# Decaying attention in a fused decoder: another order of its units, of the context's keys and values, and of the loads of the experts' results

## The chip, the cores and the metric

The kernel runs on one core of one Trainium2 chip, as a single launch. The metric is the device time of the whole launch in microseconds (us), taken as a median of several runs. A profile is one further execution of the same program, recorded by the hardware profiler: it has a span (first to last recorded instruction) and a device time of its own.

A core has five engines with a queue of their own, each of which takes its instructions strictly in order: TensorE (PE: matmul; PEld is its loading of weights), VectorE (DVE), ScalarE (ACT), GpSimd (POOL) and SyncE (SP, here only for starting transfers). SBUF is the on-chip memory with 128 partitions; PSUM holds the outputs of matmuls in a few banks. A program has to wait where one engine needs what another makes, or where a buffer is still in use.

## The reference, cut to what matters

The kernel computes a decoder of four layers on x of shape 8 x 128 x 256 (8 sequences, 128 tokens, 256 features) in float32. Each layer adds an attention, a cross attention to a context of 8 x 128 x 128 and a feed-forward part, each on the layer-normed x. The change lies where layer 1's feed-forward part (experts), layer 2's attention and the preparation of layer 2's cross attention meet:

```python
x = x + _L1_ffn_ref(_layernorm(x, axis=-1), ...)      # 8 experts, 2 for each token
x = x + _L2_attn_ref(_layernorm(x, axis=-1), L2_attn_w_qkv, L2_attn_w_out, L2_attn_decay_param)
x = x + _L2_xattn_ref(_layernorm(x, axis=-1), ctx_1024, ...)
```

Layer 2's attention has no softmax. Keys and queries go through elu + 1, and the causal sums over earlier tokens decay:

```python
q = _phi(to_bhtd(q))                                  # elu(z) + 1
k = _phi(to_bhtd(k))
decay = jax.nn.sigmoid(decay_param).reshape(1, H, 1)
running_kv = _decay_scan(k * v, decay, init)          # s_t = decay * s_{t-1} + x_t
running_ksum = _decay_scan(k, decay, init)
den = jnp.clip(jnp.sum(q * running_ksum, axis=-1, keepdims=True), EPS_DEN, None)
out = q * running_kv / den                            # 16 heads of 16 features
out = out.transpose(0, 2, 1, 3).reshape(B, T, Hid) @ w_out
```

The cross attention of layer 2 needs keys (projected from the context and normalised in each head) and values (projected from the context). Neither depends on x, so both may be made at any time before that attention starts.

## The kernel before, in words

All stages run one after the other over the same x, which stays in SBUF. Where a stage has several steps for each of its units, `in_step` (L376) writes the order of work out by hand: it takes a list of (lag, function) pairs and, at step t, calls each function in the order of the list for unit t - lag. Inside it the order of the program is the order on each engine's queue. Outside it a scheduler may move instructions; `keep_in_program_order` binds one to its place.

**End of the experts (`l1_ffn`, L1200).** For each block of 128 rows TensorE makes the expert's output, VectorE scales it (`y`, L1274) and GpSimd scatters the rows to memory (`rows_out`, L1275). GpSimd also makes the row numbers for that (`to`, L1272). When all are out, `k.l2k.keys()` is called, then eight loads of 256 KB on SyncE's queue fetch each sequence's two results for every token (`y<-rows_out`), and VectorE adds both to x (`add_x`, L192). After each half of the sequences (a group g of four) the norm's statistics are taken (`norm_stats`, `ln` L155 and `ln_mv` L156) and `xn` is written (L165).

**The context's keys (`L2Keys.keys`).** GpSimd clears `va`, the store of the values, in eight memsets (L1512) and writes two columns of ones (L1514). Then for four units u (two groups x two halves of the features) TensorE projects the keys into a "mm" bank of PSUM, ScalarE adds the bias (`kc`, L1529) and squares (`sq`, L1591), TensorE sums the squares of each head, ScalarE makes the reciprocal root (Ln and Exp, L1597 and L1598), and GpSimd multiplies `kc` by it (L1536). `rest` prepares the other constants, among them `prm`, which VectorE copies from a transposed "tr" bank (L1487).

**Layer 2's attention (`l2_attn`, L1309).** It works in four units s: group g = s // 2 (512 tokens of four sequences), half o = s % 2 (128 features, eight heads) on the partitions. First come the constants: `dec`, the decay rates; `dect` (L1325), the rates spread over tokens with a zero at the start of each sequence; `heads` and `feats` (L1343), which sum over a head's features and spread back. `k.norm()` then transposes `xn` on TensorE (`ps_tr`, L183) into `xnT` (L60 on ScalarE, L62 on VectorE). For each unit:

- `project` (TensorE, matmuls in `mm`, L46): keys, values and queries into "mm" banks, of which there are four;
- `elu` (ScalarE `e` L1363 and `z` L1364, then VectorE's `k` or `q`, L1366);
- `scan` (VectorE): `kv` L1379, the scan of the keys `rks` L1380, the scan of `kv` into `rkv` L1381;
- `weigh` (VectorE): `rks` x q L1387, `rkv` x q L1388;
- `sums` (TensorE L1396): a head's sum of `rks`, the denominators, both halves of a group in one "tr" bank;
- once for a group: `inverse` (VectorE `rec` L1403 and its reciprocal L1404), `spread` (TensorE L1411), `divided` (VectorE L1416), `output` (TensorE into "o" banks, of which there are two, then `add_x`) and the statistics of the next norm.

The list that sets the order is at the end of the function. In it, `sums` of a unit comes one step late, behind the next unit's keys and values, and `k.l2k.late` turns the finished `kc` into masked keys `kb` (ScalarE, L1564) and makes the values of two sequences (TensorE, then ScalarE `va`, L1575):

```python
in_step(
    k, NC * 2,
    (0, lambda s: project(s, 1, K)), (0, keys), (0, lambda s: project(s, 2, V)),
    (1, sums), (1, last(inverse)), (0, scan),
    (0, lambda s: project(s, 0, Q)), (1, last(spread)), (0, queries), (1, last(divided)),
    (2, last(lambda g: NORM[g]())), (0, k.l2k.late), (0, weigh), (1, last(output)), (1, last(stats)),
)
```

After it the cross attention (`l2_xattn`, L1604) starts with its own norm; GpSimd adds the bias `bo` to x (L188) as soon as `xn` has been made.

Of the kernel before, what the change touches and what calls it, by code (L numbers as in the profile page):

```python
# [17 lines left out]
P = 128  # L18
B = 8
# [29 lines left out]
class Ctx:  # L49
# [71 lines left out]
    def rsqrt_begun(self, out, x):  # L121

        nc = self.nc
        t = self.sm.tile(list(x.shape), F32, name="rs_t", bufs=4)
        nc.scalar.activation(t, x, AF.Ln)
        nc.scalar.activation(out, t, AF.Exp, scale=-0.5)

        def rest():
            nc.vector.tensor_tensor(t, out, out, ALU.mult)  # L129
            nc.vector.scalar_tensor_tensor(t, t, -0.5, x, ALU.mult, ALU.mult)  # L130
            nc.vector.scalar_tensor_tensor(out, t, 1.5, out, ALU.add, ALU.mult)

        return rest
# [10 lines left out]
    def norm_stats(self, g, table=False):  # L144
# [15 lines left out]
        begun = self.rsqrt_begun(rstd, var)  # L160
# [1039 lines left out]
def l1_ffn(k):  # L1200
# [92 lines left out]
    with k.tc.tile_pool(name="l1y", bufs=1, reuse_waits="tile") as wk_:  # L1293
        Y = [wk_.tile([P, CHOICES, D], F32, name="y2", bufs=8) for _ in range(B)]
        for b in range(B):
            at = BLOCKS + CHOICES * b * S
            nc.sync.dma_start(
                Y[b], k.rows_out[at : at + CHOICES * S, :].rearrange("(p c) d -> p c d", c=CHOICES)
            )
        for g in range(2):  # L1300
# [3 lines left out]
            k.norm_stats(g)()  # L1304
# [4 lines left out]
def l2_attn(k):  # L1309
    nc, a = k.nc, k.a  # L1310
    w = k.w6
    wqkv = w[:, 0:1536].rearrange("p (c n) -> p c n", c=NC)
    wo = w[:, 1536:2048].rearrange("p (c n) -> p c n", c=NC)
    dp = w[:, 2048:2050]
    HALF = 4 * S
    with k.tc.tile_pool(name="l2a", bufs=2, reuse_waits="tile") as wk_:

        dec = k.sm.tile([P, 2], F32, name="dec")
# [3 lines left out]
        dt_ = wk_.tile([P, NC, 4, S], F32, name="dect", bufs=1)  # L1322
        nst = k.c[:, C_NST : C_NST + S].unsqueeze(1).to_broadcast([P, 4, S])
        for o in range(NC):
            nc.vector.tensor_scalar(dt_[:, o, :, :], nst, dec[:, o : o + 1], None, ALU.mult)  # L1325

        heads = wk_.tile([P, NC, 4, 32], F32, name="heads", bufs=1)
        feats = wk_.tile([P, NC, 4, P], F32, name="feats", bufs=1)
# [10 lines left out]
        own = wk_.tile([P, 4], F32, name="own4", bufs=1)  # L1339
        nc.vector.tensor_copy(own, until)  # L1340
        nc.vector.tensor_tensor(own[:, 1:4], own[:, 1:4], until[:, 0:3], ALU.subtract)
        for o in range(NC):
# [3 lines left out]
            )  # L1346
        _, xnT = k.norm()
        K, V, Q, Z, RKV, DEN, REC, PB, PY = ({} for _ in range(9))
# [10 lines left out]
        def elu(s, of, name):  # L1359

            z = of[s]
            e, z1 = tile_("e"), tile_("z1")
# [3 lines left out]
            return lambda: nc.vector.scalar_tensor_tensor(of[s], e, 1.0, z1, ALU.min, ALU.max)  # L1366

        def keys(s):
            Z[s] = elu(s, K, "k")

        def queries(s):
            Z[s] = elu(s, Q, "q")

        def scan(s):

            dd = dt_[:, s % NC].rearrange("p b s -> p (b s)")
            kv, rkv, rks = tile_("kv", 1), tile_("rkv", 4), tile_("rks")
            Z.pop(s)()
            nc.vector.tensor_tensor(kv, V.pop(s), K[s], ALU.mult)  # L1379
            nc.vector.tensor_tensor_scan(rks, dd, K.pop(s), 0.0, ALU.mult, ALU.add)  # L1380
            nc.vector.tensor_tensor_scan(rkv, dd, kv, 0.0, ALU.mult, ALU.add)  # L1381
            RKV[s] = rkv, rks

        def weigh(s):
            rkv, rks = RKV[s]
            Z.pop(s)()
            nc.vector.tensor_tensor(rks, rks, Q[s], ALU.mult)  # L1387
            nc.vector.tensor_tensor(rkv, rkv, Q.pop(s), ALU.mult)  # L1388

        def sums(s):  # L1390
            g, o = divmod(s, NC)
            rks = RKV[s][1]
            if o == 0:
                DEN[g] = k.trt((P, P))
            for j in range(4):
# [3 lines left out]
                )  # L1399

# [5 lines left out]
        def spread(g):  # L1406
            r = REC.pop(g)
            for o in range(NC):
                PB[g, o] = k.mmt()
# [3 lines left out]
        def divided(g):  # L1413
            for o in range(NC):
                rkv = RKV[2 * g + o][0]
                nc.vector.tensor_tensor(rkv, rkv, PB.pop((g, o)), ALU.mult)  # L1416

        def output(g):
            for j in range(4):
                b = 4 * g + j  # L1420
                PY[b] = k.ot()
                mm(nc, PY[b], [(RKV[2 * g + o][0][:, tok(j)], wo[:, o, :]) for o in range(NC)])
# [5 lines left out]
        def last(f):  # L1428
            return lambda s: f(s // NC) if s % NC else None

        NORM = {}
        in_step(
            k, NC * 2,
            (0, lambda s: project(s, 1, K)), (0, keys), (0, lambda s: project(s, 2, V)),
            (1, sums), (1, last(inverse)), (0, scan),
            (0, lambda s: project(s, 0, Q)), (1, last(spread)), (0, queries), (1, last(divided)),
            (2, last(lambda g: NORM[g]())), (0, k.l2k.late), (0, weigh), (1, last(output)), (1, last(stats)),
# [3 lines left out]
class L2Keys:  # L1441
# [58 lines left out]
    def keys(self):  # L1500
# [5 lines left out]
        self.pool = pool = self.inner.enter_context(k.tc.tile_pool(name="l2kt", bufs=1, reuse_waits="tile"))  # L1506

# [3 lines left out]
        for b in range(B):  # L1511
            nc.gpsimd.memset(self.va[:, b], 0.0)  # L1512
# [8 lines left out]
        RS = {}  # L1521

        def project(u):
            g, o = divmod(u, NC)
            pk = k.mmt((P, 4, S))
# [6 lines left out]
            RS[u] = l2_rstd(k, pool, self.kc[:, u].rearrange("p b s -> p (b s)"))  # L1532

        def scaled(u):
            rs = RS.pop(u)()
            nc.gpsimd.tensor_tensor(self.kc[:, u], self.kc[:, u], rs.rearrange("p (b s) -> p b s", s=S), ALU.mult)  # L1536

        in_step(k, 4, (0, project), (1, scaled))
# [30 lines left out]
    def values(self, b):  # L1569
        k = self.k  # L1570
        pv = k.ot((P, 2, D))
        for t, wv in enumerate((self.wvm, self.wvd)):
            mm(k.nc, pv[:, t, :], [(k.ctxT[:, b, :], wv)])
        for t in range(2):
            k.nc.scalar.activation(  # L1575
                self.va[:, b, :, t, 0:16], pv[:, t, :].rearrange("p (h d) -> p h d", d=16), AF.Copy, scale=self.ends[t]
            )

    def late(self, u):
        self.masked(u)  # L1580
        for b in (2 * u, 2 * u + 1):
            self.values(b)


def l2_rstd(k, pool, t, bias=None):
# [8 lines left out]
    rs = pool.tile([P, n], F32, name="rs", bufs=2)  # L1594
# [1012 lines left out]
```

## Time and profile before

| what | value |
|---|---|
| median of three runs | 1988.71 us (1983.61, 1988.71, 1989.26) |
| the profiled execution | 1987.05 us |
| its span | 1985.0 us |
| mean granted clock of TensorE | 0.928 of full speed |
| stretch that the change touches | about 880 to 963 us of the span |

The profile's page gives the busy time of each engine over the span, then the chain of work that ended last. The trace can be asked for the same in any stretch: windows (busy time of each engine, with the TensorE clock that was granted there), the chain (start in us from the span's start, length in us, engine, tile, line), and waits (which engine's instruction waited for which, in us in total, how often, longest). "issue" is time in which an engine waited for nothing that the profile shows. A busy TensorE need not be one at full clock: in this stretch the granted clock is 0.5 from 897.99 to 911.65 and from 949.19 to 959.43 us, and 1.0 in the rest of 880 to 963. One matmul of float32 with 512 columns shows as two records; a projection is four.

Mean times of single instructions there, from the groups by line:

| instruction | engine | mean |
|---|---|---|
| `e` 128x512, `z` 128x512 | ACT | 0.60, 0.69 us |
| `va` 128x256 | ACT | 0.47 us |
| `k` and other products 128x512 | DVE | 0.67 to 0.69 us alone |
| scan 128x512 | DVE | 1.20 to 1.22 us |
| reciprocal 128x128 | DVE | 0.95 us |
| add to x 128x256 | DVE | 0.42 us |
| `kc` x root 128x512 | POOL | 1.26 to 1.44 us |
| clear of `va` 128x1024 | POOL | 0.97 us |

Instructions that follow each other on VectorE overlap a little: the next one starts 0.08 to 0.1 us before the end shown.

### The profile page before, as it was taken

What the parts mean: (1) busy time and instruction counts of PE and PEld (TensorE: products, weight loads), DVE (VectorE), ACT (ScalarE), POOL (GpSimd) and SP (SyncE); (2) the same over time, 40 slices, a digit from 0 to 9 for tenths busy, and PEclk for the clock granted to TensorE, in tenths of its full rate; (3) what the DMA queues carried; (4) which work ended last, traced back from release to release, by engine and by line L of the source; (5) the groups of instructions that cost most, each with busy time, mean ns of one, the idle gap of its engine ahead of it and who ended that gap; (6) DMA issues with size and microseconds to landing.
All of it is one profiled execution on the core that took longest, in us unless ns stands there. A gap on an engine that the chain in (4) does not pass through costs nothing.

```text
span 1985.0 us, 25197 instructions
## 1 busy us (share of the span) xinstructions
PE 1724.8 (87%) x9473; PEld 1146.6 (58%) x9479; DVE 1198.6 (60%) x2376; ACT 1035.2 (52%) x1687; POOL 419.6 (21%) x415
## 2 busy tenths in 40 slices
PE   6776977758999959998678889999999996999999
PEld 3454655535666635654356645555555556888666
DVE  5766777766677742327455576776776775445433
ACT  2446844425767731234353277787777762444422
POOL 3544623110212132340143100000000001334200
PEclk9887979879999979998888799999999998999989
DMA  3500045205000041110000021011011004000000
GB/s 133 174 25 1 1 138 186 85 0 212 6 6 11 6 165 35 49 56 19 11 1 27 8 49 33 18 33 33 17 34 32 18 1 160 1 1 1 1 1 22
DMA packets 39336, 90.02 MB, mean 45 GB/s; under 512 B 7712, under 2 KB 19872, under 8 KB 37552
## 3 DMA queue, kind: packets, MB, share of 16 engines
q1 hardware_dynamic: 31648, 69.30, 10.2%
q0 software_dynamic: 5472, 17.54, 2.9%
q8 instruction: 76, 1.25, 0.3%
q10 hardware_dynamic: 2096, 1.57, 0.2%
q14 instruction: 44, 0.36, 0.1%
HBM read 66.89 MB, written 21.51 MB: 45 GB/s over the span
## 4 chain that ended last, share of the span: by engine, by line
PE 66%; DVE 15%; ACT 11%; issue 3%; POOL 3%; DMA 2%; SPq 0%; ACTq 0%; DVEq 0%; POOLq 0%
PE ps_xz L46 9%; PE ps_o L46 7%; PE ps_o L1961 6%; PE ps_o L845 5%; PE ps_mm L46 5%; PE ps_q L46 5%; PE ps_h L46 4%; PE ps_sc L46 3%; PE ps_u L46 3%; PE ps_ty L46 2%; PE ps_xz L1878 2%; PE ps_y L46 2%; PE ps_sc L206 2%; PE ps_ty L1899 2%; DVE mx L508 2%
## 5 line engine op out<-in xcount | busy, mean ns | idle before, releaser
L46 PE MATMUL ps_xz<-xnT,wxz 128*128 128x512 f32 x512 | 236.1, 604 | 1.7 <-ACT zs L1937 1.5
L46 PEld LDWEIGHTS ps_xz<-xnT,wxz 128*128 128x128 f32 x512 | 92.8, 191 | 105.1 <-issue 101.2
L1858 DVE SCALAR_TENSOR_TENSOR xc<-pad,w,xc 128x1024 f32<-128x1024 f32 x96 | 123.0, 1282 | 28.7 <-ACT xc L1852 26.9
L1961 PE MATMUL ps_o<-wo,yg 128*128 128x256 f32 x512 | 126.3, 391 | 1.5 <-DVE yg L1940 1.5
L845 PE MATMUL ps_o<-wvo,uT 128*128 128x256 f32 x512 | 122.3, 383 | 0.0
L845 PEld LDWEIGHTS ps_o<-wvo,uT 128*128 128x128 f32 x512 | 98.4, 192 | 40.8 <-issue 30.4
L1881 ACT ACTIVATE ee<-ps_xz,sgn 128x512 f32<-128x512 f32 x128 | 87.3, 689 | 59.3 <-PE ps_xz L1878 59.2
L2239 POOL MEMSET gb<- 128x160 f32 x1 | 0.2, 231 | 504.2 <-PE ps_ty L46 504.2
L1961 PEld LDWEIGHTS ps_o<-wo,yg 128*128 128x128 f32 x512 | 92.3, 189 | 24.8 <-issue 12.8
L1901 DVE TENSOR_TENSOR dtx<-ps_ty,dt 128x512 f32<-128x512 f32 x64 | 41.4, 687 | 84.2 <-PE ps_ty L1899 84.0
L46 PE MATMUL ps_h<-moe,xT 128*128 x184 | 85.0, 606 | 0.9 <-DVE xT L1241 0.7
L1891 DVE TENSOR_TENSOR ee<-ee,gT 128x2048 f32<-128x2048 f32 x32 | 73.2, 2288 | 12.4 <-ACT ee L1887 12.4
L952 POOL TENSOR_TENSOR s<-s,sums 128x512 f32<-128x512 f32 x32 | 33.3, 1040 | 207.6 <-DVE sums L951 66.3
L46 PE MATMUL ps_u<-pT,cx 128*128 128x512 f32 x128 | 70.1, 630 | 6.8 <-ACT pT L828 6.7
L944 ACT ACTIVATE s<-ps_sc,mx,rqs 128x128 f32<-128x128 f32 x128 | 48.1, 456 | 49.8 <-DVE rs_t L129 46.9
L1887 ACT ACTIVATE ee<-ee,sgn 128x1024 f32<-128x1024 f32 x64 | 73.1, 1146 | 0.2
L206 PE MATMUL ps_sc<-kb,qT 32*128 32x256 f32 (+1 forms) x384 | 44.8, 575 | 29.8 <-DVE mx L508 10.0
L509 POOL TENSOR_TENSOR s<-s,mx 128x2048 f32<-128x2048 f32 x16 | 57.8, 3610 | 53.2 <-DVE mx L508 53.2
L1255 DVE TENSOR_TENSOR h<-ps_h,sl 128x512 f32<-128x512 f32 x23 | 15.9, 692 | 82.3 <-PE ps_h L46 82.3
L46 PE MATMUL ps_ty<-ee,dtx 128*64 128x128 f32 x1024 | 63.0, 276 | 3.0 <-DVE ee L1891 3.0
L46 PEld LDWEIGHTS ps_q<-xnT,wqk 128*128 128x128 f32 x512 | 63.5, 196 | 2.8 <-DVE xnT L62 1.0
L46 PE MATMUL ps_q<-xnT,wqk 128*128 128x128 f32 x512 | 64.0, 280 | 0.6 <-DVE xnT L62 0.6
(576 smaller groups left out, 4120.2 us busy)
## 6 DMA issues: line engine op xcount, KB each, us to landing
moe<-in_p SPq DMA_DIRECT2D x24, 512.0 KB
rows_in<-zero_rows POOLq DMA_DIRECT2D x1, 8385.0 KB, 34.4
wxz<-in_p9s SPq DMA_DIRECT2D x32, 256.0 KB
fold_vo<-in_p SPq DMA_DIRECT2D x8, 512.0 KB
wvo<-fold_out SPq DMA_DIRECT2D x16, 256.0 KB
wvo<-wvo SPq DMA_DIRECT2D x2, 2048.0 KB
wo<-in_p9s SPq DMA_DIRECT2D x16, 256.0 KB
st<-in_p SPq DMA_DIRECT2D x3, 1024.0 KB
```

The lines of the kernel that those rows point to most:

```text
L46: nc.tensor.matmul(out, lhsT, rhs, start=(i == 0), stop=(i == len(pairs) - 1))
L206: k.nc.tensor.matmul(psc(r, n), q[rows], rhs, start=True, stop=True)
L508: nc.vector.tensor_reduce(mx, SC.pop(u).rearrange("p r (j t) -> p (r j) t", t=P), AX.X, ALU.max)
L509: nc.gpsimd.tensor_tensor(sv, sv, mx.unsqueeze(2).to_broadcast([P, 16, P]), ALU.subtract)
L845: k.nc.tensor.matmul(self.po[b], uT[:, j, :], self.wvo[:, 4 * hg + j, :], start=hg + j == 0, stop=hg + j == 6)
L944: nc.scalar.activation(s[:, j, :], psc[:, j, :], AF.Exp, scale=rs[:, j : j + 1], bias=mx[:, j : j + 1])
L1858: nc.vector.scalar_tensor_tensor(XC[n], (PAD[n] if n in PAD else pads[n % 2])[:, :, t : t + S], cw[:, n, t : t + 1], XC[n], ALU.mult, ALU.add)
L1881: nc.scalar.activation(e, pm, AF.Relu, scale=sgn[:, at : at + 1])
L1887: nc.scalar.activation(EE[n][:, h], EE[n][:, h], AF.Exp, scale=sgn[:, at : at + 1])
L1891: nc.vector.tensor_tensor(EE[n], EE[n], gT.unsqueeze(1).to_broadcast([P, 2, B, S]), ALU.mult)
L1901: nc.vector.tensor_tensor(DTX[n][:, bs], pt.rearrange("p (b h d) -> p b h d", b=4, d=HD), dt_[:, bs, 2 * n : 2 * n + 2].unsqueeze(3).to_br ...
L1961: nc.tensor.matmul(PO[b // 2][:, b % 2 * D : (b % 2 + 1) * D], YG[n][:, tok(b)], WO[n // 2][:, n % 2, :], start=False, stop=n == 31 and b ...
```

## The change

- **Loads of the results.** Four loads of two sequences each (512 KB) take the place of eight of one (256 KB). `norm_stats` gets a flag that binds its small Ln on ScalarE to its place.
- **Constants of the decay.** A class `Decay` makes `dec`, `dect`, `heads`, `feats` and `own4` at the start of `L2Keys.keys`, ahead of the loads; `l2_attn` only reads them.
- **GpSimd's order.** The eight clears of `va` are bound to the program's order, behind the last scatter and behind `heads`.
- **The context's steps.** Keys and values are made by the same five stages (project, values, squares, values_out, scaled) on "o" banks of PSUM. Units 0 and 1 run inside `keys`, units 2 and 3 inside the first two steps of `l2_attn`. Before, all four units of keys ran in `keys` and all values in `l2_attn`.
- **The attention's order.** At each step keys, queries and values of unit s are projected one after the other; `sums`, `inverse`, `spread`, `divided` and `output` of the unit before come after that. VectorE's work on a unit moves to the step after its projections and is split: `weights` (`k`, the scan of the keys, `q`, `rks` x q) comes first, then `scan` (`kv` and its scan), then `inverse` of the group, then `weigh`. `spread` takes "tr" banks; `rks` has one buffer instead of two, `rkv` three instead of four, `e` and `z1` three instead of two.

The diff, with unchanged code cut:

```diff
--- before.py
+++ after.py
@@ -118,11 +118,13 @@
-    def rsqrt_begun(self, out, x):
-        nc.scalar.activation(t, x, AF.Ln)
+        ins = nc.scalar.activation(t, x, AF.Ln)
+        if keep:
+            self.tc.keep_in_program_order(ins)
...
@@ -1291,41 +1293,44 @@
-        Y = [wk_.tile([P, CHOICES, D], F32, name="y2", bufs=8) for _ in range(B)]
-        for b in range(B):
+        Y = []
+        for b in range(0, B, 2):
+            y = wk_.tile([P, 2, CHOICES, D], F32, name="y2", bufs=4)
             at = BLOCKS + CHOICES * b * S
             nc.sync.dma_start(
-                Y[b], k.rows_out[at : at + CHOICES * S, :].rearrange("(p c) d -> p c d", c=CHOICES)
+                y, k.rows_out[at : at + 2 * CHOICES * S, :].rearrange("(n p c) d -> p n c d", p=S, c=CHOICES)
             )
+            Y += [y[:, 0], y[:, 1]]
...
-            k.norm_stats(g)()
+            k.norm_stats(g, keep=True)()
...
+class Decay:
+    def __init__(self, k, pool):
+        nc = k.nc
+        dp = k.w6[:, 2048:2050]
...
-        dt_ = wk_.tile([P, NC, 4, S], F32, name="dect", bufs=1)
+        self.rates = tile_("dect", NC, 4, S)
...
-            nc.vector.tensor_scalar(dt_[:, o, :, :], nst, dec[:, o : o + 1], None, ALU.mult)
-        heads = wk_.tile([P, NC, 4, 32], F32, name="heads", bufs=1)
-        feats = wk_.tile([P, NC, 4, P], F32, name="feats", bufs=1)
+            nc.vector.tensor_scalar(self.rates[:, o, :, :], nst, dec[:, o : o + 1], None, ALU.mult)
+        heads, feats = self.heads, self.feats = tile_("heads", NC, 4, 32), tile_("feats", NC, 4, P)
...
-        own = wk_.tile([P, 4], F32, name="own4", bufs=1)
+        own = tile_("own4", 4)
...
+def l2_attn(k):
...
+    dt_, heads, feats = k.decay.rates, k.decay.heads, k.decay.feats
+    with k.tc.tile_pool(name="l2a", bufs=2, reuse_waits="tile") as wk_:
         _, xnT = k.norm()
...
@@ -1359,37 +1374,32 @@
         def elu(s, of, name):
-            e, z1 = tile_("e"), tile_("z1")
+            e, z1 = tile_("e", 3), tile_("z1", 3)
...
             of[s] = tile_(name)
-            return lambda: nc.vector.scalar_tensor_tensor(of[s], e, 1.0, z1, ALU.min, ALU.max)
+            Z[s, name] = lambda: nc.vector.scalar_tensor_tensor(of[s], e, 1.0, z1, ALU.min, ALU.max)
         def keys(s):
-            Z[s] = elu(s, K, "k")
+            project(s, 1, K)
+            elu(s, K, "k")
         def queries(s):
-            Z[s] = elu(s, Q, "q")
-        def scan(s):
+            project(s, 0, Q)
+            elu(s, Q, "q")
+        def weights(s):
             dd = dt_[:, s % NC].rearrange("p b s -> p (b s)")
-            kv, rkv, rks = tile_("kv", 1), tile_("rkv", 4), tile_("rks")
-            Z.pop(s)()
-            nc.vector.tensor_tensor(kv, V.pop(s), K[s], ALU.mult)
-            nc.vector.tensor_tensor_scan(rks, dd, K.pop(s), 0.0, ALU.mult, ALU.add)
-            nc.vector.tensor_tensor_scan(rkv, dd, kv, 0.0, ALU.mult, ALU.add)
-            RKV[s] = rkv, rks
-        def weigh(s):
-            rkv, rks = RKV[s]
-            Z.pop(s)()
+            rks = RKV[s] = tile_("rks", 1)
+            Z.pop((s, "k"))()
+            nc.vector.tensor_tensor_scan(rks, dd, K[s], 0.0, ALU.mult, ALU.add)
+            Z.pop((s, "q"))()
             nc.vector.tensor_tensor(rks, rks, Q[s], ALU.mult)
-            nc.vector.tensor_tensor(rkv, rkv, Q.pop(s), ALU.mult)
         def sums(s):
             g, o = divmod(s, NC)
-            rks = RKV[s][1]
+            rks = RKV[s]
             if o == 0:
                 DEN[g] = k.trt((P, P))
             for j in range(4):
@@ -1398,6 +1408,17 @@
                     start=o == 0, stop=o == 1, skip_group_check=True,
                 )
+        def scan(s):
+            dd = dt_[:, s % NC].rearrange("p b s -> p (b s)")
+            kv, rkv = tile_("kv", 1), tile_("rkv", 3)
+            nc.vector.tensor_tensor(kv, V.pop(s), K.pop(s), ALU.mult)
+            nc.vector.tensor_tensor_scan(rkv, dd, kv, 0.0, ALU.mult, ALU.add)
+            RKV[s] = rkv
+        def weigh(s):
+            nc.vector.tensor_tensor(RKV[s], RKV[s], Q.pop(s), ALU.mult)
...
-                PB[g, o] = k.mmt()
+                PB[g, o] = k.trt((P, 512))
...
         def divided(g):
             for o in range(NC):
-                rkv = RKV[2 * g + o][0]
+                rkv = RKV[2 * g + o]
                 nc.vector.tensor_tensor(rkv, rkv, PB.pop((g, o)), ALU.mult)
...
+        def other_half(f):
+            return lambda s: f(s + 2) if s < 2 else None
         in_step(
             k, NC * 2,
-            (0, lambda s: project(s, 1, K)), (0, keys), (0, lambda s: project(s, 2, V)),
-            (1, sums), (1, last(inverse)), (0, scan),
-            (0, lambda s: project(s, 0, Q)), (1, last(spread)), (0, queries), (1, last(divided)),
-            (2, last(lambda g: NORM[g]())), (0, k.l2k.late), (0, weigh), (1, last(output)), (1, last(stats)),
+            (0, keys), (0, queries), (0, lambda s: project(s, 2, V)),
+            (1, weights), (1, sums), (1, scan), (1, last(inverse)), (1, last(spread)), (1, weigh),
+            (1, last(divided)), (2, last(lambda g: NORM[g]())), (1, last(output)), (1, last(stats)),
+            (0, k.l2k.masked), *((lag, other_half(f)) for lag, f in k.l2k.stages),
         )
@@ -1504,12 +1527,13 @@
+        k.decay = Decay(k, pool)
...
         for b in range(B):
-            nc.gpsimd.memset(self.va[:, b], 0.0)
+            k.tc.keep_in_program_order(nc.gpsimd.memset(self.va[:, b], 0.0))
...
+        PK, SQ, V = {}, {}, {}
         def project(u):
-            pk = k.mmt((P, 4, S))
+            pk = k.ot((P, 4, S))
...
-            RS[u] = l2_rstd(k, pool, self.kc[:, u].rearrange("p b s -> p (b s)"))
+            SQ[u] = pool.tile([P, 512], F32, name="sq", bufs=2)
+            nc.scalar.activation(SQ[u], self.kc[:, u].rearrange("p b s -> p (b s)"), AF.Square)
+        def values(u):
+            for b in (2 * u, 2 * u + 1):
+                pv = V[b] = k.ot((P, 2, D))
+                for t, wv in enumerate((self.wvm, self.wvd)):
+                    mm(nc, pv[:, t, :], [(k.ctxT[:, b, :], wv)])
+        def values_out(u):
+            for b in (2 * u, 2 * u + 1):
+                pv = V.pop(b)
+                for t in range(2):
+                    nc.scalar.activation(
+                        self.va[:, b, :, t, 0:16], pv[:, t, :].rearrange("p (h d) -> p h d", d=16), AF.Copy,
+                        scale=self.ends[t],
+                    )
+        def squares(u):
+            pv = PK[u] = k.ot((P, 512))
+            mm(nc, pv, [(k.c[:, C_BO16 : C_BO16 + P], SQ.pop(u))])
         def scaled(u):
-            rs = RS.pop(u)()
+            rs = l2_root(k, pool, PK.pop(u))()
             nc.gpsimd.tensor_tensor(self.kc[:, u], self.kc[:, u], rs.rearrange("p (b s) -> p b s", s=S), ALU.mult)
-        in_step(k, 4, (0, project), (1, scaled))
+        self.stages = (0, project), (0, values), (1, squares), (0, values_out), (1, scaled)
+        in_step(k, 2, *self.stages)
...
-    def values(self, b):
-        k = self.k
-        pv = k.ot((P, 2, D))
...
-    def late(self, u):
-        self.masked(u)
-        for b in (2 * u, 2 * u + 1):
-            self.values(b)
...
+    return l2_root(k, pool, pv)
+def l2_root(k, pool, pv):
+    nc = k.nc
+    rs = pool.tile(list(pv.shape), F32, name="rs", bufs=2)
```

## The prediction

> **What bounds the kernel now.** I read the page first: is the span made of arithmetic or of transfers, and on which engine does the last chain run.
>
> ```profile
> span 1985.0 us, 25197 instructions
> ...
> PE 1724.8 (87%) x9473; PEld 1146.6 (58%) x9479; DVE 1198.6 (60%) x2376; ACT 1035.2 (52%) x1687; POOL 419.6 (21%) x415
> ...
> PE 66%; DVE 15%; ACT 11%; issue 3%; POOL 3%; DMA 2%; SPq 0%; ACTq 0%; DVEq 0%; POOLq 0%
> ```
>
> TensorE carries two thirds of the chain, but the edit touches only about 82 us of 1985, so the average says little. The windows view, cut where the chain changes its engine, gives that stretch (us, then busy time of each engine, granted clock, DMA):
>
> ```profile
> core 0: us, PE busy (x) PEld busy (x) DVE busy (x) ACT busy (x) POOL busy (x), PEclk, DMA share, GB/s
> 880.20:891.60 11.40, 8.76 (x34) 5.46 (x34) 1.95 (x6) 6.52 (x13) 8.80 (x11) 1.00 0.26 84
> 891.60:906.90 15.30, 6.57 (x19) 3.64 (x20) 15.22 (x51) 6.37 (x14) 4.81 (x6) 0.71 0.26 93
> 906.90:928.40 21.50, 21.50 (x74) 11.24 (x73) 13.54 (x20) 13.50 (x28) 0.00 (x0) 0.89 0.00 0
> 928.40:939.20 10.80, 9.86 (x46) 7.32 (x47) 9.33 (x16) 4.72 (x11) 0.00 (x0) 1.00 0.01 2
> 939.20:962.70 23.50, 16.44 (x74) 11.14 (x73) 15.54 (x32) 6.08 (x15) 3.41 (x4) 0.78 0.00 0
> ```
>
> Five regimes: the last scatter and the round trip of its rows; VectorE adding and normalising (15.22 of 15.30 busy); TensorE without a gap; VectorE and TensorE mixed; then a tail in which neither is full. The chain over the same stretch names the links that the edit touches (start, length):
>
> ```profile
> 881.71 1.08 POOL va L1512 x2
> ...
> 884.61 1.04 POOL rows_out L1275
> ...
> 888.00 3.63 DMA y<-rows_out
> ...
> 903.53 1.17 DVE dect L1325
> ...
> 910.49 1.50 PE ps_tr L183 x8
> ...
> 951.82 0.70 PE ps_tr L1396 x8
> ```
>
> The last of these is the second group's denominators. In the waits view of 906 to 963, TensorE's one long wait stands just before them, and it is on VectorE:
>
> ```profile
> PE ps_tr L1396 <- DVE rks L1387: 5.7, 1, 5.7
> ...
> DVE rec L1403 <- PE ps_tr L1396: 1.8, 2, 1.7
> ```
>
> So in the front VectorE's order decides, in the middle the number of TensorE's matmuls, in the tail how much VectorE has in its queue ahead of the last `rks`. These are the three things that the change reorders.
>
> **Part 1, the front.** GpSimd: the last scatter waited behind three clears of `va` (881.71 to 884.45); its rows were ready at 882.73 + 0.80, the lag of the steady loop. With the clears behind it, it starts at 883.53, 1.08 earlier. The eight 256 KB loads landed at 891.62, 892.28, then about 0.66 apart until 896.33; four of 512 KB start when a pair is complete, so the first add moves from 891.65 to 892.28 - 1.08 = 891.2: a gain of only 0.45. `dect` (1.17 + 0.37 on the chain) moves into VectorE's idle time before 891: -1.5.
>
> Against that stand three things. (a) The scaling of `kc` on GpSimd now falls on the dense adds. In before, the pair starting 893.55 and 900.84 stretched one add from 0.42 to 1.08 (+0.67) and one `xn` from 0.40 to 1.35 (+0.95), 1.6 in all. [...] I take 1.9, because adds follow each other there but statistics (one input) stand between; against before's 1.6 that is +0.3. (b) The copy of `prm` (L1487), which frees a "tr" bank of PSUM, is queued on VectorE behind the second group's statistics, so the first transposes start about 903.6, no earlier than before's 903.0. (c) All sixteen transposes go before the first projection: the second eight, 1.50 in the chain at 910.49, come ahead of it at half clock, 1.7. So the first projection starts about 908.1 instead of 906.9: **+1.2**. [...]
>
> **Part 2, first projection to `rec` of group 0.** TensorE is full here, so matmuls are counted. One projection is four records, 1.72 at full clock, 3.41 at half. Before: eight of them ahead of the denominators (one at half: 3.41 + 7 x 1.72 = 15.5), transposes 1.50, values 2 x 1.73, denominators 0.36 + 0.40: 21.2, the chain's 907.08 to 928.41. After: keys, queries and values of units 0, 1 and 2 stand ahead of unit 1's denominators, so nine (17.2); context steps 2 and 3 bring project 0.87 + values 1.73 each (5.2) and one sum of squares (0.9); denominators 0.8; transposes gone: 24.1. Context products now share the two "o" banks, each freed by ScalarE (`va` 0.47 each, `kc` 0.84 a pair, where `e` 0.60 and `z` 0.68 queue too): about 0.3 to 0.7 at each of three places, 1.2. Sum 25.3: `rec` goes from 928.44 to about 933.9, +5.4 with the front. VectorE has unit 1 finished at about 928 and then waits some 5.5 in its queue at `rec`: unit 2's work is behind it.
>
> **Part 3, `rec` to group 0's last add.** Before 928.44 to 939.18, 10.7, with 3.4 + 1.9 of unit 2's VectorE work in between. After: `rec` and reciprocal 1.3, spread's eight records 1.1 to the first half, division, output, four adds at 0.87: 7.7. Ends about 941.6: **+2.4 so far**; three microseconds came back.
>
> **Part 4, the tail.** Unit 2's VectorE work has only been put off. Before, 939.18 to the last denominators at 951.82 is 12.6: statistics 2.35, a wait 1.57, unit 3's `k`, `kv` and two scans 3.65, norm 0.57 + 2.19, `q` and `rks` x `q` 2.2. After: statistics 2.3; all of unit 2 (`k` 0.7, scan 1.14, `q` 0.7, product 0.6, `kv` 0.7, scan 1.2, weigh 0.6 = 5.7, +0.8 for the last `kc` product beside a scan); norm 0.6 + 2.6 (GpSimd's x + bo beside it, as before); unit 3's `k`, scan, `q`, product 3.6 (one stretched): 15.6. That is +3.0; the denominators start about 957.1. Behind them on VectorE stand unit 3's `kv` and scan (1.8) before `rec`, of which the denominators cover 0.7: +1.0. [...] TensorE's projections for unit 3 are done by 947 and hidden. Last add: 962.24 + 2.4 + 3.0 + 1.0 = 968.6. The instructions that follow keep their order and start from that add.
>
> **Sum.** +1.2 + (4.2 - 3.0) + 3.0 + 1.0 = **+6.4 us**. The profiled execution took 1987.05 (span 1985.0 and 2.05 around it): 1993.5. The median, 1988.71, lies 1.66 above: **1995.0**. A difference of 0.3%, 6 us, is about what a measurement of this kernel can tell from no change.
>
> **The rivals.**
> [...] Chance 0.20.
> (R2) ScalarE becomes the bound: `sq`, Ln, Exp and `kc` of two context steps (about 3 each) stand in front of `e` and `z` in its queue, and TensorE, waiting for banks, loses one or two windows at full clock (1.7 each). +10: 1998.7. For it: ScalarE is busy 13.50 of 21.50 there. Against: the moved steps give up 1.4 of `va` each. Chance 0.16.
> (R3) The reorder costs, but GpSimd's products meet nothing (-1.9, -0.8) and banks wait half as long: +3: 1991.7. Chance 0.12.
> The likeliest case, 0.52, has its own range of +4 to +9, 1992.7 to 1997.7.
>
> **How the numbers follow.** Slower by over 0.3%: R2 (0.16) and the likeliest above +6 (0.40), 0.56. Within: R3 (0.12), the likeliest below +6 (0.12), R1's greater part (0.13), 0.37. Faster: R1 if the tail's VectorE queue is also hidden, 0.07. The range for 8 in 10 leaves out the lower half of R1 and R2's end: 1985.5 to 2000.
>
> **What would show it.** Right: last scatter at about 883.5, first add 891.2, first projection at 907 to 909; an idle time of about 5 us on VectorE before the first `rec`, released by TensorE's denominators; TensorE idle 9 us or more before the last denominators, released by the `rks` product; last add of the stage 966 to 970. Wrong: a VectorE that is busy before the first `rec`, a front that starts its projections by 905, or a tail in which TensorE's wait is not longer than 5.7.

## The result and the profile after

The changed kernel takes 2000.73 us in the median, the kernel before 1988.03 in the same comparison: a ratio of 1.0052, 95% interval 1.0038 to 1.0066, or 10.3 us more (the ratio is estimated from all the runs; the two medians alone are 12.7 apart). Its profiled execution took 1998.94:

```profile
span 1997.2 us, 25198 instructions
...
PE 1726.3 (86%) x9479; PEld 1147.0 (57%) x9479; DVE 1205.8 (60%) x2376; ACT 1036.0 (52%) x1687; POOL 420.1 (21%) x415
```

The work is the same, so the 12.2 us between the spans are waiting and clock. Each VectorE instruction can be followed from one trace to the other. The shift is -1.08 at the experts' last `y`, +6.38 at the attention's last add to x, +9.1 after the next stage with its routing, +9.34 until 1880 us and +12.4 in the last 102 us. So the stretch that was edited costs 7.46 from the last `y` on, and 2.7 more are lost in the stage behind it. The last 3.05 turned out to be chance (e9 below), and the -1.08 ahead of the edit is taken for chance too: in the 13 profiles that last `y` starts anywhere from 878.4 to 884.4. The windows view of the changed kernel, cut at the same events as before's, except that its first row starts at the last `y` and before's 2.05 us ahead of it (columns as there: length, busy PE, PEld, DVE, ACT, POOL, clock, DMA share, GB/s):

```profile
881.20:891.60 10.40, 8.47 (x36) 5.28 (x34) 8.35 (x12) 6.63 (x17) 9.05 (x12) 1.00 0.49 165
891.60:908.30 16.70, 5.28 (x22) 3.89 (x22) 15.79 (x54) 3.53 (x9) 3.79 (x4) 0.66 0.09 33
908.30:933.70 25.40, 24.68 (x79) 11.69 (x78) 10.73 (x13) 18.59 (x37) 1.27 (x1) 0.96 0.00 0
933.70:941.60 7.90, 6.43 (x34) 5.28 (x35) 4.84 (x10) 0.00 (x0) 0.00 (x0) 1.00 0.01 2
941.60:969.00 27.40, 14.88 (x67) 9.70 (x67) 21.97 (x40) 7.65 (x16) 4.68 (x5) 0.75 0.00 0
```

Row by row against before: from the last `y` to the first add it takes 10.43 instead of 9.40, so the wait for the results is no shorter, and VectorE is now busy in it for 8.35 us instead of 1.95. The middle grew from 21.5 to 25.4, with ScalarE at 18.59 where it had 13.50. The fourth row is 2.9 shorter, and VectorE's work missing there (4.84 instead of 9.33) turns up in the tail (21.97 instead of 15.54). The chain and the waits name the links:

```profile
886.52 5.16 DVE bvT L1597 x2
...
891.68 2.59 DVE x L194 x4
...
903.71 0.06 DVE prm L1510
...
903.81 1.98 PE ps_tr L185 x8
...
933.28 0.40 PE ps_tr L1406 x8
...
947.75 2.31 DVE rkv L1416
```

```profile
PE ps_tr L1406 <- DVE rks L1398: 9.9, 1, 9.9
...
DVE rec L1424 <- PE ps_tr L1406: 5.6, 1, 5.6
```

TensorE's wait before the last denominators went from 5.7 to 9.9, VectorE's at `rec` from 1.7 to 5.6, both as forecast. New is `bvT`: two small instructions (a constant of the next stage) that hold VectorE for 5.16 us just ahead of the first add.

All runs on one table, each from its own profile: last `y` of the experts to the first add of results; from there to the attention's first projection; from there to the end of its last add; their sum; the next stage (from there to the first `top` of the routing behind it); and the ratio of the timed runs to before. Rows without a ratio are single executions. All but before, its repetition, the delayed one and e10 have the second group's transposes ahead of the first projection, where they take 1.8. The expectations count the changed kernel's first projection from 908.49; its first matmul is at 908.28, so their 60.55 is 60.76 here.

| kernel | y to add | to projection | to last add | sum | next stage | ratio, interval |
|---|---|---|---|---|---|---|
| before | 9.40 | 15.22 | 55.79 | 80.41 | 136.34 | 1 |
| before, second profile (e9) | 9.25 | 15.22 | 55.85 | 80.32 | 136.26 | |
| before, delayed (e11) | 9.53 | 15.22 | 57.39 | 82.14 | 138.04 | |
| changed | 10.43 | 16.67 | 60.76 | 87.87 | 139.05 | 1.0052, 1.0038 to 1.0066 |
| e1: `bvT` on ScalarE | 8.35 | 16.14 | 60.33 | 84.82 | 138.73 | 1.0029, 1.0017 to 1.0042 |
| e2: attention's order back | 10.44 | 16.67 | 63.96 | 91.07 | 139.33 | 1.0074, 1.0060 to 1.0088 |
| e3: both | 8.32 | 16.14 | 63.31 | 87.78 | 139.01 | 1.0059, 1.0045 to 1.0073 |
| e4: two `rks` | 10.44 | 16.67 | 60.74 | 87.85 | 139.06 | |
| e5: sums first | 10.43 | 16.67 | 58.27 | 85.38 | 138.10 | 1.0044, 1.0030 to 1.0057 |
| e6: context's steps back | 10.43 | 17.85 | 56.37 | 84.65 | 139.19 | 1.0041, 1.0025 to 1.0056 |
| e7: only the front | 8.29 | 17.87 | 53.95 | 80.10 | 136.49 | 0.9996, 0.9987 to 1.0006 |
| e8: e6, sums first | 8.47 | 17.40 | 52.47 | 78.34 | 138.37 | 1.0004, 0.9994 to 1.0014 |
| e10: third order | 8.49 | 14.55 | 47.52 | 70.56 | 139.79 | 0.9965, 0.9953 to 0.9977 |

Sum and next stage together explain the timed runs: against before they give +10.2 for the changed kernel (measured 10.3), +6.8 for e1 (5.8), +13.7 for e2 (14.7), +10.0 for e3 (11.7), +6.7 for e5 (8.8), +7.1 for e6 (8.2), -0.2 for e7 (-0.8), 0.0 for e8 (0.8) and -6.4 for e10 (-7.0); each lies within the interval of its ratio. The intervals of the changed kernel, e1, e5 and e6 overlap; these four are told apart by the stages of their profiles.

### The profile page after: what moved, and what is told of

The parts are those of the page before. It is cut to its first block, busy times and chain, and to the rows that moved or that the text cites. A ratio compares the mean times of both kernels' runs of the same rounds, so it can differ in the third digit from the quotient of the medians.

```text
span 1997.2 us, 25198 instructions
## 1 busy us (share of the span) xinstructions
PE 1726.3 (86%) x9479; PEld 1147.0 (57%) x9479; DVE 1205.8 (60%) x2376; ACT 1036.0 (52%) x1687; POOL 420.1 (21%) x415
## 3 DMA queue, kind: packets, MB, share of 16 engines
q1 hardware_dynamic: 31584, 69.30, 10.1%
q8 instruction: 76, 1.25, 0.2%
## 4 chain that ended last, share of the span: by engine, by line
PE 66%; DVE 15%; ACT 11%; issue 3%; POOL 2%; DMA 2%; SPq 0%; ACTq 0%; DVEq 0%; POOLq 0%
PE ps_xz L46 9%; PE ps_o L46 7%; PE ps_o L1997 6%; PE ps_o L847 5%; PE ps_mm L46 5%; PE ps_q L46 5%; PE ps_h L46 4%; PE ps_sc L46 3%; PE ps_u L46 3%; PE ps_ty L46 2%; PE ps_y L46 2%; PE ps_xz L1914 2%; PE ps_sc L208 2%; PE ps_ty L1935 2%; DVE mx L510 2%
```

## The experiments

**e1: is the first add late because of `bvT`?**

```diff
-            nc.vector.tensor_scalar(bv[:, o], k.ones, self.prm[:, 4 + o, 0:1], self.prm[:, 4 + o, 1:2], ALU.mult, ALU.add)
+            nc.scalar.activation(bv[:, o], k.ones, AF.Identity, bias=self.prm[:, 4 + o, 1:2], scale=self.prm[:, 4 + o, 0:1])
```

> The changed kernel with one edit: the two bvT instructions (constants of the next stage) are made by ScalarE instead of VectorE. Measure: from the start of the last y to the end of the attention's last add to x; before 80.41 us (882.25 to 962.66), after 87.87 (881.17 to 969.04). Theory: in the changed kernel VectorE stood 5 us in bvT while GpSimd's clears of va ran back to back, so the first add came at 891.60 although the first pair of loads had its data by about 888.9; with bvT away the first add comes 2.0 to 2.5 earlier against the last y (8.1 after it instead of 10.4) and the measure is 85.4 to 86. Rival: the loads set the first add, bvT only filled the wait: first add and measure unchanged (87.5 to 88.2). Whole time by the theory about 2 us under the changed kernel, some 8 over before.

The timeline of GpSimd in the changed kernel, and of VectorE in e1 (start, length, what; in brackets the idle time before it and what ended it):

```profile
884.34 7.20 POOL L1536 MEMSET va<- 128x1024 f32 x8
```

```profile
892.10 1.43 DVE L194 TENSOR_TENSOR x<-y,x 128x256 f32<-128x256 f32 x4 [3.24 <-DMA y<-rows_out]
```

The clears run from 884.34 to 891.54, and `bvT` ends with the last of them; in e1 VectorE is idle and the loads end its wait, 2.08 earlier against the last `y`. The sum is 84.82 instead of 87.87, even 0.6 below what was expected, since the way to the first projection shortened by 0.5 too. The rival fell. In before the same two instructions stood beside one last clear, which ended at 884.45, and took 0.71:

```profile
883.89 0.71 DVE L1552 TENSOR_SCALAR bvT<-consts,prm 128x128 f32<-128x128 f32 x2
```

In all eight profiles in which VectorE makes `bvT`, its first instruction ends 0.08 us after the last of the back-to-back clears, whether that is the third (before) or the eighth.

**e2 and e3: the attention's order of before in the changed kernel, without and with e1's edit.**

```diff
-            (0, keys), (0, queries), (0, lambda s: project(s, 2, V)),
-            (1, weights), (1, sums), (1, scan), (1, last(inverse)), (1, last(spread)), (1, weigh),
-            (1, last(divided)), (2, last(lambda g: NORM[g]())), (1, last(output)), (1, last(stats)),
-            (0, k.l2k.masked), *((lag, other_half(f)) for lag, f in k.l2k.stages),
+            (0, keys), (0, lambda s: project(s, 2, V)),
+            (1, sums), (1, last(inverse)), (0, scan),
+            (0, queries), (1, last(spread)), (0, lambda s: elu(s, Q, "q")), (1, last(divided)),
+            (2, last(lambda g: NORM[g]())),
+            (0, k.l2k.masked), *((lag, other_half(f)) for lag, f in k.l2k.stages),
+            (0, weigh), (1, last(output)), (1, last(stats)),
```

> The changed kernel with the attention's order of before (keys and values, sums of the unit before, scans of both in the same step, then queries; two rks, four rkv, spread in the mm banks), all else as changed: early constants, four loads, the context's steps split. Measure: first projection to the last add, before 55.8 us (906.87 to 962.66), after 60.55 (908.49 to 969.04). Theory: the order of the attention alone costs these 4.7; expected 55.5 to 56.5, with VectorE's wait at the first rec under 2 and TensorE's wait before the last denominators near 5.7. Rival: the context's project and squares on ScalarE and GpSimd inside the attention cost it: 58 to 60. Whole time by the theory 4 to 5 under the changed kernel, about +3 to +5 over before because of the front.

> Both edits of the two kernels sent with it: bvT on ScalarE and the attention's order of before. Theory: the two losses add up, so taking both away gives a measure from the last y to the last add of 80.5 to 81.5 us (before 80.41, after 87.87), and a whole time within 3 us of before. Rival of another kind, that what follows the stretch loses 3 to 6 us because of the change itself and not by the chance of the clock's windows: whole time 3 to 6 over before although the measure is equal.

My theory fell: with before's order the attention takes 63.96, longer than with the new one. The waits of e2 between 905 and 976 say why:

```profile
DVE rec L1420 <- PE ps_tr L1413: 8.8, 2, 8.7
...
PE ps_o L46 <- ACT kc L1551: 4.2, 2, 2.1
```

TensorE stands twice for 2.1 us, waiting for an "o" bank that ScalarE's `kc` has to empty, and `kc` is queued behind `e`, `z` and the masked keys. That is e2's rival, the context's steps inside the attention, and more than the 58 to 60 that it was given; these two waits are 4.2 of it. In e3, `bvT` gave 2.1 again up to the first add and 3.3 in all, so the two edits do not add up to before's time: 87.78 instead of 81.

**e4: two buffers for `rks`** (`tile_("rks")` in place of `tile_("rks", 1)`).

> The changed kernel with two buffers for rks instead of one. In it the scan of unit 1's keys waited 1.9 us for unit 0's sums, which stand behind unit 1's projections. Theory: VectorE waits for the first rec anyway (5.6 us), so the wait only moves there: first projection to last add 60.3 to 61.2 (60.76). Rival: the wait is on the path: 58.5 to 59.5.

60.74 against 60.76: VectorE's wait of 1.9 was covered by its wait at `rec`.

**e5: sums and inverse ahead of the next projections.**

```diff
-            (0, keys), (0, queries), (0, lambda s: project(s, 2, V)),
-            (1, weights), (1, sums), (1, scan), (1, last(inverse)), (1, last(spread)), (1, weigh),
+            (1, weights), (1, sums), (1, last(inverse)),
+            (0, keys), (0, queries), (0, lambda s: project(s, 2, V)),
+            (1, scan), (1, last(spread)), (1, weigh),
```

> The changed kernel with one reorder in the attention's list: the denominators' products, their sums and the inverse of the unit before stand ahead of the next unit's projections; scan, spread and weigh stay behind them. Theory: the first rec comes at about 928 instead of 933.7, but its spread still waits for three projections (5.2), so group 0 gains some 1.5 to 2; in the tail rec no longer stands behind kv and its scan (1.8), gain 1 to 1.7. First projection to last add 57 to 58 instead of 60.55. Rival: TensorE waits for the rks product ahead of its projections and loses what is gained: 60 to 61.5.

58.27, a gain of 2.5: most of what was expected, though 0.3 outside the range (57 to 58). The rival fell.

**e6: the context's steps back, the new order kept.** All four units of keys again ahead of the attention and `(0, k.l2k.late)` in its list.

> The changed kernel with the context's steps as before: all four units of keys ahead of the attention (in mm banks), only masked keys and values inside it; attention's order, constants, loads and GpSimd's order as changed. First projection to last add: before 55.8 us, changed kernel 60.8, changed with the attention's order of before 64.0. Theory: the two units of context keys inside the attention are what costs (ScalarE's kc, sq and roots ahead of the bank that TensorE waits for): expected 55.5 to 57, so that the changed order alone costs nothing to 1.2. Rival: the order costs by itself (unit 2's work behind rec): 59 to 61.

56.37: the theory held for the context's steps; that the order would then cost at most 1.2 did not. Together with e7, which has before's order too, four kernels give a square of the attention's time, all with the new constants and loads: 53.95 with neither, 56.37 with the new order alone, 63.96 (63.31 in e3) with the context's steps inside alone, 60.76 with both. The context's steps cost 4.4 in the new order and 9 to 10 in the old. The new order by itself cost 2.4, of which up to 0.7 may belong to `bvT` and `prm`, which e7 alone of these four has on ScalarE (moving `bvT` there gave 0.4 in e1 and 0.7 in e3). The three parts close the account from before to the changed kernel: 53.95 is 1.8 under before's 55.79, by what the second group's transposes take, which moved to the front; then +2.4 and +4.4 give 60.76. In the front the split gave back 1.2 (17.85 to 16.67).

**e7 and e8: the front alone, and the front with e5's order.** Both have the context's steps as before, `bvT` and `prm` on ScalarE.

> Attention's order and context's steps as before; early constants, GpSimd's order and four loads as changed; bvT and prm (constants of the next stage) made by ScalarE, so that VectorE meets no clear and the first transposes no queue. Theory: first add 8.3 us after the last y (before 9.40), first projection 14.5 to 16 after that with four GpSimd products beside the adds, first projection to last add 54 to 55.8. Last y to last add 77.5 to 79.5, 1 to 3 under before's 80.4; whole time 1 to 3 under before. Rival: what follows the attention loses some 3 us in every kernel with the new front, whatever the stretch does: whole time 0 to 2 over before.

> As the kernel before it, but with the changed attention's order in which denominators, their sums and the inverse stand ahead of the next unit's projections (that edit gave 2.5 us in the changed kernel). Theory: if the context's keys are the cost, first projection to last add 53 to 55, last y to last add 76.5 to 79: the best of all. Rival (order costs by itself): 57 to 59 and 81 to 83.

e7 equals before, and 1 to 3 less were expected; e8 has the shortest sum so far, 2.1 under before, and loses it again in the next stage (138.37). In both the way to the first projection took 17.4 to 17.9 instead of 14.5 to 16. The timeline of e8, VectorE and then ScalarE:

```profile
897.23 0.37 DVE L160 TENSOR_SCALAR ln_var<-ln_mv 128x4 f32<-128x4 f32 x1
```

```profile
902.91 0.19 ACT L125 ACTIVATE rs_t<-ln_var 128x4 f32<-128x4 f32 x1
```

The variance of the first group is ready at 897.6, its Ln starts at 902.9: bound to its place in the program (`keep=True`), it stands behind the `sq` and the roots of all four units. With two units in the front, as in the changed kernel, that queue is short. The binding and the split belong together, which I had not seen. (In e10, which has the Ln unbound, the way to the first projection is 14.55 instead of e8's 17.40; 1.8 of that are the second group's transposes, which there come later.)

**e9: before, profiled once more.**

> The kernel before, unchanged, once more, for a second profile. In the profiles so far the part from the attention's last add to the end of the next stage's routing took 136.3 in before and 138.1 to 139.3 in the five others, and the last 102 us 102.3 in before and 105.3 in all others. If that is chance of the clock's windows in the one profile of before, this run shows values near the others (138 to 139, 105.3) or in between; if it is made by the change, 136.3 and 102.3 again.

One of each: 136.26 again, but 105.34. So the last 3.05 us were chance of one profile (in all 13 profiles that part takes either 102.3 or 105.3, and 102.3 in before and e11 alone), and the 2.7 of the next stage were not.

**e11: before with 2.4 us of useless products ahead of the last `rec`.**

```diff
         def inverse(g):
+            if g == 1:
+                idle = tile_("idle", 1)
+                for _ in range(4):
+                    nc.vector.tensor_tensor(
+                        idle, dt_[:, 0].rearrange("p b s -> p (b s)"), dt_[:, 1].rearrange("p b s -> p (b s)"), ALU.mult
+                    )
```

> The kernel before with 2.4 us of needless VectorE work (four products that nobody reads) ahead of the last rec of the attention; it leaves nothing out. A test of the next stage's time, which was 136.3 us twice in before and 136.5 with the attention of before, but 138.1 to 139.3 in all kernels whose attention ended otherwise. In the first three the last add ended 3.2 to 3.3 us after an edge of the clock's 3.41 us windows, in the others 0.3 to 1.5. Theory: only this position matters; the delay moves the last add by 1 to 2 us, that is to 0.5 to 1.8 behind an edge, and the next stage takes 138 to 139.3. Rival: the changed constants or order act on the next stage itself: 136.3.

The next stage alone, in the windows view of before, of the changed kernel and of e11; the number to look at is the clock, third from the end:

```profile
962.70:1099.00 136.30, 102.06 (x716) 73.21 (x714) 67.54 (x143) 60.92 (x75) 54.08 (x68) 0.81 0.05 15
```

```profile
969.00:1108.10 139.10, 104.55 (x717) 75.22 (x714) 67.45 (x144) 60.86 (x75) 54.08 (x68) 0.79 0.05 15
```

```profile
963.80:1101.90 138.10, 103.46 (x717) 74.80 (x714) 67.40 (x144) 60.95 (x75) 54.10 (x68) 0.80 0.05 15
```

The same instructions, the same busy time on the other engines, but TensorE was granted less. In all 13 traces the granted clock is 0.5 or 1.0 and changes only at edges 3.41 us apart; the stretch from one edge to the next is a window. The last add of before ended 3.23 after an edge (959.43), of e9 3.20, of e7 3.27: next stage 136.3 to 136.5. In all others it ended 0.3 to 1.6 after one, and the next stage took 138.0 to 139.8, with 54 to 58 us at half clock instead of 51. In e11 nothing but the delay was added, the position became 1.61, and the stage took 138.04. So the position does it, and not what the change does to the stage.

The table holds more than that. Add to each next stage the time by which the last add lies behind an edge: 136.34 + 3.23 in before, 139.05 + 0.50 in the changed kernel, 138.73 + 0.91 in e1, 138.04 + 1.61 in e11. The sum is 139.5 to 139.8 in 11 of the 13 profiles (140.1 in e6 and e10). In these 11 the stage therefore ends at a fixed distance from the edge ahead of the last add, wherever in its window that add lies. The last `y`, too, starts 1.3 to 1.7 after an edge in all 13. So from the last `y` to the routing a kernel gains or loses whole windows: +3 in the changed kernel (10.17 us; three are 10.24), +2 in e1 and e5, +4 in e2, +3 in e3, +1 in e11, 0 in e7 and e8 and, within half a microsecond, +2 in e6 and -2 in e10. This is why e8's 2.07 were lost again, and why a delay of 1.73 in e11 cost 3.43.

**e10: a third order.** e8 with the small Ln unbound, two buffers for `rks`, four for `rkv`, and this list:

```diff
+            (1, sums), (1, last(inverse)), (1, scan), (1, weigh),
+            (0, keys), (0, queries), (0, lambda s: project(s, 2, V)), (1, last(spread)),
+            (0, weights), (1, last(divided)), (2, last(output)), (0, k.l2k.late),
+            (3, last(stats)), (4, last(lambda g: NORM[g]())),
```

> A version meant to beat both: the new front (constants early, last scatter ahead of the clears, four loads, bvT and prm on ScalarE, the norm's small Ln free of the program's order, since in the kernel sent before it waited 5 us behind the context's roots), the context's steps as before, and a third order of the attention: denominators, sums and inverse of the unit before stand first; then the three projections; VectorE's work on k and q in the same step as its projections (so unit 2's lies ahead of group 0's adds, in the time that VectorE waited for rec's spread); output of group 0 behind unit 3's projections. Theory (VectorE's queue in the tail is what sets the end): first projection to last add 46 to 50 us (before 55.8, best so far 52.5), last y to last add 72 to 75 (before 80.4); the next stage starts with one norm more, so 1 to 3 are given back; whole time 3 to 7 under before. Rival (TensorE's total work sets it): no better than 52, whole time equal to before.

The last three windows (first projection to first `rec`, to group 0's last add, to the end) and one wait:

```profile
905.10:922.40 17.30, 17.28 (x65) 9.36 (x66) 11.40 (x18) 11.51 (x25) 0.00 (x0) 0.92 0.00 0
922.40:940.80 18.40, 18.40 (x76) 11.39 (x76) 15.32 (x22) 10.99 (x22) 0.00 (x0) 1.00 0.00 1
940.80:952.60 11.80, 7.71 (x46) 5.57 (x44) 8.53 (x21) 2.08 (x6) 0.00 (x0) 1.00 0.00 0
```

```profile
DVE rec L1426 <- PE ps_tr L1408: 2.8, 2, 1.7
```

TensorE is without a gap until the last denominators, and at full clock from 907.93 to the end; VectorE does unit 2 while it used to wait. The sum is 9.9 below before (70.56, where 72 to 75 were expected), the next stage takes 3.4 back (its position is 0.34, and the first norm now follows the last add), and the whole is faster than both kernels: 0.9965.

## Why the prediction was right in direction and short in size

Slower was forecast, by 6.4 us, and it became slower by 10.3. That is outside the likeliest case's own range of 4 to 9 and at the end of the wide one: the median, 2000.73, lies just past its 2000, and the ratio on before's 1988.71 gives 1999.05. Times are taken from the last `y`, to leave out the 1.08 by which the profiled run was ahead there.

- **Part 1, to the first projection: forecast +1.2, measured +2.5.** The failed step is "the first add moves from 891.65 to ... 891.2: a gain of only 0.45". It came 1.03 later. The loads were early enough (e1: 8.35 after `y`); VectorE was not free. I had listed what the moved clears release on GpSimd's queue and not who meets them there: `bvT`, which the change never names, and which I had costed nowhere. Without it the gain would have been 1.05 (e1), more than the 0.45. The other terms held. The 1.9 for the two `kc` products was my own estimate, and no run shows it: in before two of them made 1.6, and here the products stretched two adds from 0.42 to 1.48 and 1.15, 1.8 in all. And `prm` released the transposes at 903.81, which is 904.9 with the 1.08 put back; 903.6 was forecast, and the difference is what the first add was late.
- **Part 2, projection to `rec`: forecast 4.2 more, measured 3.85** (21.57 to 25.42). VectorE idled 5.6 (5.5 forecast). That 25.3 came out so near is partly luck: TensorE's work was 24.7 instead of 24.1, and the waits for banks 0.6 instead of 1.2.
- **Part 3: forecast -3.0, measured -2.8** (10.74 to 7.92).
- **Part 4: forecast +3.0 and +1.0, measured +3.4 and +1.0** (12.64 to 16.01; denominators to `rec` 0.72 to 1.73). The `rkv` scan at 947.75 is the one that the last `kc` product stretched, by 1.1 instead of 0.8. From the second `rec` on, for which the sum has no term, it took 9.7 instead of 10.1; the granted clock was 0.5 there until 965.13, in before until 959.43.
- **Behind it: forecast 0, measured +2.7.** "The instructions that follow keep their order and start from that add" is true, and still they ran longer. I had not weighed the clock for the stage that comes after it. As e11 shows (a delay of 1.73 cost 3.43), its end follows the edges and not the last add, so the cost was rounded up to three windows. By the same count (an estimate from before's position 3.23 and the sum of 139.57) the forecast 6.4 would have put the last add 2.8 after an edge and cost 6.8, two windows: the 1.1 that the stretch took beyond 6.4 carried it over one more edge and cost 3.4.

Parts 2 to 4 together were forecast at 5.2 and measured at 5.0. The two missing terms, 1.3 in the front and 2.7 behind, are what lay between 6.4 and 10.2. None of the rivals took place as told. R1, at 0.20 the case of a TensorE at full clock up to its first projections, did not come: the granted clock was 0.5 from 896.86 to 910.51. R2's sum of +10 is near by luck: its mechanism (ScalarE in front of the banks) was a part of what I had counted as 1.2, and TensorE's own gaps in the middle are 0.7 (25.40 less 24.68), and no window (3.41 us from edge to edge; the 1.7 of R2 is half of one) went to half clock for them: the granted clock was 1.0 from 910.51 to 951.47. R3's banks that wait half as long did come, but not its products that meet nothing. The square of e6 and e7 adds one thing: of the loss in the attention 4.4 goes to the context's steps moved into it and only about 2.4 to the order.

What stays open: which instructions of the next stage take up the difference, so that it ends at the same distance from an edge, was not taken apart; nor why e6 lies 0.5 off that rule; and e10's own next stage mixes position and the later norm.

## What to carry to other kernels

Work that is moved to fill a wait has to be looked at from the engine that it meets there, also by instructions that the change does not touch: ask of each moved instruction who else runs at that time. Before a producer's order is changed, look at which engine's queue has the last word in the tail (here VectorE's): e10's order, with unit 2's work ahead of group 0's adds, made the attention 4.9 shorter than e8's, where its front gave 1.6 against before. (Part of the 4.9 is the norm that moved behind the last add, and no run has unit 2's place alone.) And a difference of a few microseconds can have a part in a stage that nobody edited: here a gain counted only when it carried the next stage over an edge of the clock (e8's 2.07 up to the last add were lost again by 138.37 in the next stage). Compare stage by stage, look at where a stage's end lies between two edges, and repeat the profile of before, to tell place from chance.

## What the runs showed of the hardware

Two small VectorE instructions (`bvT`, 128x128, one SBUF input and two scalars; the shorter of the two took 0.45 us in before, and ScalarE makes each in 0.48 to 0.51) were held for 5.16 us by clears on GpSimd, which read nothing. They were let go only when the eighth of the back-to-back clears had ended, not between two of them. `feats` and `prm`, which read PSUM, ran beside the same clears in their usual 0.69 and 0.17, and in e1 the adds, with two SBUF inputs, ran beside the last clears in 0.42. `bvT` began beside the third clear and was not let in at any of the five changes from one clear to the next. What kept it waiting there no run here shows. Before's trace had the hint already: beside `kc` products two more tensor_scalar instructions with one SBUF input were stretched, an `xn` from 0.40 to 1.35 and `dect` from 0.45 to 1.25.

The second surprise was how a stage's end is tied to the clock's edges: before's last add lay 3.23 and 3.20 after an edge in two runs whose edges differ by 1.35 us against the program's start, and the next stage's `top` came 2.9 to 3.2 after an edge in 11 of the 13 profiles (0.1 to 0.2 in e6 and e10).
